# A graph-attention and aggregation kernel: words gathered ahead of a scatter, last tiles turned between products, dense tiles finished between the last gathered ones

## The chip, the cores and the metric

The kernel runs on one core of one Trainium2 chip. The metric is the device time of one execution in microseconds (us). Engines are named as the profile names them: PE (TensorE, matrix products; PEld are its weight loads), DVE (VectorE), ACT (ScalarE), POOL (GpSimd, which here issues all indirect DMAs) and SP (SyncE, which here only issues DMAs). Each engine works through its own instructions in the order written; they meet at semaphores.

## What is computed

Two layers over 4096 nodes with 512 features. The adjacency matrix is 4096 x 4096, symmetric, with about one entry in 500 and the diagonal set. Layer 0 is an attention in which each head takes only its best neighbour; layer 1 is a mean over the neighbours with two linear maps.

```python
h = maximum(layernorm(x), 0)
Q, K, V = h @ WQ.T, h @ WK.T, h @ WV.T            # 8 heads of 64
attn = softmax(Q K^T / 8 + Q @ we.T + be, where adj > 0)
hard = (attn == max(attn, axis=-1)) / 8
x = x + hard @ V

h = maximum(layernorm(x), 0)
agg = mask(adj) @ h / maximum(degree, 1)
self_f, nb_f = h @ W_self + b_self, agg @ W_nb + b_nb
x = x + relu(concatenate([self_f, nb_f]) @ W_comb + b_comb)
```

## The kernel before

Every row of the adjacency matrix is first packed into 256 words of 16 bits; the set bits are decoded into lists of neighbours, and the nodes are sorted by degree into 32 tiles of 128 rows (`perm` holds the permutation). Tile 0 has the nodes of highest degree; `CAPS` holds the length of the longest list of each tile, the node itself included, from 24 for tile 0 to 8 for tile 23, 7 for tiles 24 to 27, 6 for 28 to 30 and 5 for 31. The work has three stages, and in all of them the order of instructions on each engine is the order in which the program writes them (`manual_schedule`).

**First stage** (the first gather of key rows starts at 346.9 us): keys, values, packed words and lists of all tiles.

**Second stage** (to about 1072 us): a loop over `i` from -5 to 31 that takes one tile per round in the order `turns`, which ends with 29, 30, 31. POOL gathers the key rows of the tile's neighbours (L1103), DVE multiplies them with the query and picks the best neighbour of each head (`scores`, `winners`), and the result goes through layer 1's normalisation on ACT (`layer1_stats`, `layer1_norm`), is turned by four PE transposes (`layer1_turn`, into `tr`), copied by ACT (L1347, for the tail L1509), multiplied with the two folded weights on PE, and one product `pg` (= h W_nb W_comb of the tile) is copied by ACT to `gs` and scattered by POOL into the DRAM tensor `G_d` (L1119). The other product goes into `own`, which SP stores with `xo` in `X1_d`. A planner (`plan`) sets in which round each step of each tile comes. The last five tiles, 15, 28, 29, 30 and 31, have no round left for their products; they are the `tail`. For these the steps are: `layer1_turn` (PE), `tail_turn` (ACT copy into `room`, L1509), `tail_product` (PE, eight records of `pg`, L628), `tail_move` (ACT copy to `gs`, L1519, then POOL's scatter). Tiles 15, 28 and 29 are turned in round 30 and multiplied in round 31 (`early`), tile 30 is turned in round 31 and tile 31 after the loop. In round 30 POOL also gathers the packed words of the seven densest tiles (`dense_words`, seven indirect DMAs from `W_d`); they are turned on PE after the loop into `wT`. After that the `own` products of the tail follow.

**Third stage** (from about 1072 us): the neighbour sums of layer 1, in two ways side by side. For the seven *dense* tiles (0 to 6) PE multiplies a 0/1 mask with all of `G`, in 16 planes of 14 products each: per plane DVE unpacks a mask `mk` from `wT` (L1643, three buffers), ACT's queue loads a slab `gk` of `G_d` (three buffers), and PE adds into seven PSUM tiles `da` (L1662). In the last plane the products are sorted by tile, so that tile 0 is complete first. For the *gathered* tiles 7 to 31 POOL gathers the rows of `G_d` of all neighbours (L1103, `CAPS` - 1 gathers of 128 rows, into one of three parts of `room`), and DVE adds them up (`total`, L1684; for tile 31 `halved`, L1693). `finish` is two DVE instructions (L1674, L1675) that scale the sum, add the own product, apply the relu and add x; it reads the tile of `X1_d` that SP loaded (L1669, twelve buffers that are used in turn). `put` is POOL's scatter of a finished tile to the output (L1119); two puts in a row have a small memset between them (L1118). Before the change POOL puts one tile in each round after the round's gathers, and always leaves the latest in the list `done`. Masks are emitted at a pace of one per 13 rows of lists; mask 14 follows tile 23's finish and mask 15 tile 25's, each ahead of the next tile's sum. The seven dense tiles are finished at the end: tiles 0 to 2 after tile 30's sum, before tile 31's, and tiles 3 to 6 after it.

Of the kernel before, what the change touches and what calls it, by code (L numbers as in the profile page):

```python
# [515 lines left out]
DENSE = 7  # L516
# [21 lines left out]
def sparse_path(  # L538
# [553 lines left out]
    with ExitStack() as pb:  # L1092
# [403 lines left out]
        def late(step, kind, i, *args):  # L1496

            out_ = []
            for r in turns:
                if plan[kind].get(r) == i:  # L1500
                    out_ += step(r, *args) or []
            return out_
# [22 lines left out]
        for i in range(-5, KT):  # L1525


            if i == -3:
                load_fold(0)
            if i == 0:  # L1530
                load_bias()
            if i == 1:
                wS = wp.tile([P, NC, D], F32, tag="w_b", name="swS")
                wN = bp.tile([P, NC, D], F32, tag="swN", name="swN", bufs=1)
            a, b = on(key_gathers, i), late(value_gathers, "value", i)
            while a or b:
                for q, n in ((a, max(1, round(len(a) / max(1, len(b))))), (b, 1)):
                    for g in q[:n]:
                        gather(*g)
                    del q[:n]  # L1540
            on(rows, i + 5)
            late(layer1_move, "move", i)
            on(query_copy, i + 2)
            late(layer1_copy, "layer1", i)
            early = [r for r in tail if plan["turn"][r] == i - 1]
            for r in early:
                tail_turn(r)
            if i >= 0 and turns[i] in fused:
                own_values(turns[i])
            late(layer1_stats, "stats", i)  # L1550
            on(query_norm, i + 4)
            on(query, i + 1)
            for part in between.get(i, ()):
                fold(*part)
            late(layer1, "layer1", i)
            for r in early:
                tail_product(r)
            if i in (-2, -1, 0):
                n = 2
                for t in late_v[:n]:  # L1560
                    w = values_out(t, values(t, psm), bp, nc.sync)
                    for g in beyond:
                        tc.declare_no_dep(w.ins, g.ins, reason="other columns")
                    written.append(w)
                del late_v[:n]
            if i == max(between) + 1:
                fold_bias()

            def within():
                late(layer1_inverse, "stats", i)  # L1570
                late(layer1_out, "move", i)

            if i >= 0:
                scores(turns[i], within)
            late(scatter, "move", i)
            if i == KT - 2:
                wg = dense_words()
                gsl = [gp.tile([P, GRP, D], F32, tag="kg", name="gs") for _ in range(2)]
            on(winners, i)
            late(layer1_norm, "stats", i)  # L1580
            on(query_turn, i + 3)
            late(layer1_turn, "turn", i)
            for r in early:
                tail_move(r)

        late(layer1_xo, "stats", KT)
        for r in tail:
            if plan["turn"][r] == KT - 1:
                tail_turn(r)
                tail_product(r)  # L1590
        late(layer1_stats, "stats", KT, True)
        late(layer1_norm, "stats", KT)
        for r in tail:
            if plan["turn"][r] == KT - 1:
                tail_move(r)
        for r in tail:
            if plan["turn"][r] == KT:
                layer1_turn(r)
                tail_turn(r)
                tail_product(r)  # L1600
                tail_move(r)


        over = bp.tile([P, KT], F32, tag="over", name="over", bufs=1)
# [26 lines left out]
    with ExitStack() as pd:  # L1631
        dp = pd.enter_context(tc.tile_pool(name="sd", bufs=4))
        gp = pd.enter_context(tc.tile_pool(name="sdg", bufs=3))
        psd = pd.enter_context(tc.tile_pool(name="spsd", bufs=1, space=PSUM))
        order = pd.enter_context(ExitStack())
        order.enter_context(tc.manual_schedule())
        dacc = [psd.tile([P, D], F32, tag=f"da{r}", name="da") for r in range(DENSE)]
        masks, keys = {}, {}

        def dense_mask(s):  # L1640

            mk = gp.tile([P, 2, DENSE, P], F32, tag="mk", name="mk")
            nc.vector.tensor_scalar(  # L1643
                mk.rearrange("p h b q -> p (h b q)").bitcast(I32),
                wT.rearrange("p h b q -> p (h b q)"), 22 - s, 0x40000000,
                ALU.logical_shift_left, ALU.bitwise_and,
            )
            masks[s] = mk

        def dense_keys(s):  # L1650
            gk = gp.tile([P, 2, D], F32, tag="gk", name="gk")
            nc.scalar.dma_start(
                gk, G_d[ds(s * SEG, SEG), :].rearrange("(h p) f -> p h f", p=P)
            )
            keys[s] = gk

        def dense_sum(s):
            todo = [(h, r) for h in range(2) for r in range(DENSE)]
            if s == NPL - 1:
                todo.sort(key=lambda hr: hr[1])  # L1660
            for h, r in todo:
                nc.tensor.matmul(  # L1662
                    dacc[r], masks[s][:, h, r, :], keys[s][:, h, :],
                    start=(s == 0 and h == 0), stop=(s == NPL - 1 and h == 1),
                )

        def load_x1(r):
            x1 = dp.tile([P, 2, D], F32, tag="x1", name="x1", bufs=DENSE + 5)
            nc.sync.dma_start(x1, X1_d[ts(r, P), :, :])  # L1669
            return x1  # L1670

        def finish(r, acc, by, x1):
            x1, y = x1[:, 0, :], x1[:, 1, :]
            nc.vector.scalar_tensor_tensor(y, acc, by, y, ALU.mult, ALU.add)  # L1674
            nc.vector.scalar_tensor_tensor(y, y, 0.0, x1, ALU.max, ALU.add)  # L1675
            done.append((r, y))

        def put():
            put_rows(out[:, :], *done.pop(0))

        def total(g, n):

            acc = dp.tile([P, D], F32, tag="acc", name="acc", bufs=2)
            nc.vector.tensor_reduce(  # L1684
                acc, g[:, 0:n, :].rearrange("p n f -> p f n"), AX.X, ALU.add
            )
            return acc

        def halved(g, n):

            while n > 1:
                h = n // 2
                nc.vector.tensor_tensor(  # L1693
                    g[:, 0:h, :], g[:, 0:h, :], g[:, n - h : n, :], ALU.add
                )
                n -= h
            return g[:, 0, :]


        half = cp.tile([P, DENSE], F32, tag="half", name="half")  # L1700
        nc.vector.tensor_scalar(half, smeta[:, 0:DENSE, M_RD - M_DEG], 0.5, None, ALU.mult)
        done = []
        puts.clear()
        for s in range(NPL):
            dense_keys(s)
        ahead = 3
        for s in range(ahead):
            dense_mask(s)
            dense_sum(s)
        s = ahead  # L1710
        calls = 0

        pace = 13
        x1s = {}
        for r in range(DENSE, KT):
            n = CAPS[r] - 1
            for q in [*range(r, min(r + 4, KT)), *(range(DENSE) if r == KT - 2 else ())]:
                if q not in x1s:
                    x1s[q] = load_x1(q)
            gg = room[:, ds(r % 3 * GMAX * D, GMAX * D)].rearrange("p (n f) -> p n f", f=D)  # L1720
            for i in range(n):
                gather(gg[:, i, :], G_d[:, :], sidx[:, r, i + 1 : i + 2])
            if len(done) > 1:
                put()
            if r == KT - 1:

                for k in range(DENSE // 2):
                    finish(k, dacc[k], half[:, k : k + 1], x1s.pop(k))
                    put()
            acc = (total if r < KT - 1 else halved)(gg, n)  # L1730
            finish(r, acc, smeta[:, r, M_RD - M_DEG : M_RD + 1 - M_DEG], x1s.pop(r))
            calls += n + 1
            while s < NPL and calls >= pace * (s - 2):
                dense_mask(s)
                dense_sum(s)
                s += 1
        while done:
            put()
        for k in range(DENSE // 2, DENSE):
            finish(k, dacc[k], half[:, k : k + 1], x1s.pop(k))  # L1740
            put()
        order.close()
    return nc.values_load(fi[0:1, 0:1], min_val=0, max_val=P)  # L1743
# [46 lines left out]
```

## Time and profile before

| | |
|---|---|
| median of 5 runs | 1429.41 us (1425.88 to 1443.62) |
| the profiled execution | 1414.95 us |
| its span, first to last instruction | 1413.1 us |
| first gather of G (third stage) | at 1072.70 us |
| first mask of the dense products | at 1110.27 us |
| PE's last dense product ends | at 1377.7 us |
| DVE's last finish ends, POOL's last put starts | at 1400.20, 1400.48 us |

The rows of a timeline give the start and the duration in us, the engine, the line, the operation with the tile it writes and those it reads, the shapes, the count of instructions that are merged in the row, and in brackets the idle time of the engine before it with what ended that. "issue" means that nothing in the profile shows what the engine waited for, "remote" a release by something that could not be named. A product of 128x512 in float32 leaves two records on PE. Starts and ends of PE records are not exact: the record is that of the issue, and the end is modelled.

### The profile page before, as it was taken

Reading aid. Unit: us, or ns where it says so; the run is one execution under the profiler, and the core shown is the slowest. Engines: PE = TensorE matmul, PEld = TensorE weight load, DVE = VectorE, ACT = ScalarE, POOL = GpSimd, SP = SyncE. Lnnn points to the kernel's source line nnn. Section 1 sums busy time; section 2 is a strip of 40 time slices with the busy share of each in tenths; the row PEclk is TensorE's granted clock in tenths of the full one; section 3 lists DMA queues with packets and bytes.
Section 4 is the critical chain, followed back from the end, with each engine's and each line's share of the span. In section 5 each row is a group of like instructions: output and inputs, shape, how many; then the busy total and the mean of one; then the engine's idle time right before and its main releaser. Section 6 shows DMA issues by size and latency. Waiting matters only on the chain. (4 is left out here: it accounts for less than half of the span.)

```text
span 1413.1 us, 10657 instructions
## 1 busy us (share of the span) xinstructions
PE 1045.1 (74%) x2852; PEld 475.9 (34%) x2852; DVE 997.7 (71%) x1651; ACT 427.7 (30%) x880; POOL 782.6 (55%) x918
## 2 busy tenths in 40 slices
PE   5998989858772648567787757777789397887590
PEld 3554545423330223223332223333333143333140
DVE  5468786884594398778877787777572577688395
ACT  5787776612100333232333323332530000000000
POOL 2222313233677476666766666667345475767474
PEclk9999999979985769778887888888899698979595
DMA  9999998296765376777777777767555896778673
GB/s 364 419 420 421 420 361 304 109 352 218 210 202 152 97 240 216 227 233 244 224 229 225 221 226 225 225 208 223 209 175 173 306 332 220 256 253 276 206 235 124
DMA packets 109973, 352.57 MB, mean 249 GB/s; under 512 B 18208, under 2 KB 18208, under 8 KB 101712
## 3 DMA queue, kind: packets, MB, share of 16 engines
q0 software_dynamic: 64128, 210.72, 47.3%
q1 hardware_dynamic: 39552, 129.78, 23.8%
q10 hardware_dynamic: 6224, 11.31, 2.3%
q8 instruction: 24, 0.39, 0.1%
q14 instruction: 45, 0.37, 0.1%
HBM read 287.74 MB, written 68.19 MB: 252 GB/s over the span
## 5 line engine op out<-in xcount | busy, mean ns | idle before, releaser
L1662 PE MATMUL da<-gk,mk 128*128 128x512 f32 x448 | 215.0, 633 | 67.9 <-issue 45.6
L628 PE MATMUL q<-wq,hqT 128*128 128x512 f32 x256 | 147.8, 691 | 120.7 <-issue 100.0
L1103 POOL DMA_INDIRECT room<-G_d,sidx x184 | 184.3, 1002 | 57.8 <-issue 54.8
L1103 POOL DMA_INDIRECT kg<-K_d,sidx x177 | 169.9, 960 | 75.8 <-issue 54.3
L1227 DVE TENSOR_REDUCE sc<-pr 128x32 f32<-128x2048 f32 (+3 forms) x114 | 183.3, 1608 | 3.9
L1684 DVE TENSOR_REDUCE acc<-room 128x512 f32<-128x4096 f32 (+5 forms) x24 | 161.1, 6713 | 7.6 <-DMA room<-G_d,sidx 6.5
L628 PE MATMUL pg<-swN,hT 128*128 128x512 f32 x216 | 127.9, 747 | 45.2 <-ACT hT L1347 40.1
L1662 PEld LDWEIGHTS da<-gk,mk 128*128 128x128 f32 x448 | 90.2, 202 | 192.8 <-issue 192.8
L1103 POOL DMA_INDIRECT o<-K_d,vi x128 | 123.6, 966 | 39.2 <-issue 38.7
L628 PE MATMUL pk<-wk,room 128*128 128x512 f32 x256 | 118.3, 605 | 4.5 <-ACT room L810 4.4
L1103 POOL DMA_INDIRECT room<-K_d,sidx x102 | 99.3, 974 | 32.9 <-issue 26.8
L628 PE MATMUL pv<-wv,room 128*128 128x512 f32 x256 | 116.8, 608 | 0.0
L628 PEld LDWEIGHTS q<-wq,hqT 128*128 128x128 f32 x256 | 51.9, 213 | 184.9 <-issue 179.6
L1224 DVE TENSOR_TENSOR pr<-q,kg 128x2048 f32<-128x2048 f32 (+3 forms) x51 | 102.4, 2007 | 1.3
L1360 PE MATMUL pr<-swS,hT 128*128 128x512 f32 x216 | 99.9, 605 | 0.0
L1224 DVE TENSOR_TENSOR pr<-q,room 128x2048 f32<-128x2048 f32 (+3 forms) x42 | 66.8, 1590 | 41.1 <-issue 26.5
L628 PEld LDWEIGHTS pg<-swN,hT 128*128 128x128 f32 x216 | 50.9, 244 | 129.6 <-issue 69.7
L1119 POOL DMA_INDIRECT G_d<-gs,perm x32 | 31.8, 993 | 101.9 <-ACT gs L1366 68.4
L1366 ACT COPY gs<-pg 128x512 f32<-128x512 f32 x27 | 15.7, 583 | 223.2 <-remote 134.7
L749 ACT ACTIVATE mkt<-adjt,sgb 128x2048 bf16<-128x2048 int32 x37 | 74.2, 2006 | 13.3 <-POOL adjt L670 13.1
L1260 DVE COPY_PREDICATED o<-best,room 128x512 f32<-128x512 int32 x102 | 74.3, 729 | 4.6 <-DVE o L1260 1.1
L824 POOL DMA_DIRECT2D K_d<-ks x32 | 18.8, 587 | 100.8 <-DVE ks L819 98.6
(222 smaller groups left out, 1537.1 us busy)
## 6 DMA issues: line engine op xcount, KB each, us to landing
adjt<-adj_dram SPq DMA_DIRECT2D x37, 1024.0 KB
room<-adj_dram SPq DMA_DIRECT2D x27, 1024.0 KB
x<-X_d SPq DMA_DIRECT2D x32, 512.0 KB
xt<-x_dram SPq DMA_DIRECT2D x32, 256.0 KB
K_d<-ks POOLq DMA_DIRECT2D x32, 256.0 KB
X_d<-xo SPq DMA_DIRECT2D x32, 256.0 KB
X_d<-own SPq DMA_DIRECT2D x32, 256.0 KB
gk<-G_d ACTq DMA_DIRECT2D x16, 512.0 KB
```

The lines of the kernel that those rows point to most:

```text
L628: nc.tensor.matmul(dst, h[:, c, :], w[:, c, :], start=(c == 0), stop=(c == NC - 1))
L749: nc.scalar.activation(mk, st[t]["adj"][j], AF.Sigmoid, bias=sgb, scale=400.0, accum_out=degs[:, t, j : j + 1],)
L824: nc.gpsimd.dma_start(K_d[ts(t, P), D : 2 * D], ks)
L1103: last[0] = nc.gpsimd.indirect_dma_start(out=dst, out_offset=None, in_=src, in_offset=bass.IndirectOffsetOnAxis(ap=idx, axis=0), element_o ...
L1119: new = nc.gpsimd.indirect_dma_start(out=dst, out_offset=bass.IndirectOffsetOnAxis(ap=perm[:, r : r + 1], axis=0), in_=src, in_offset=None,)
L1224: nc.vector.tensor_tensor(pr[:, :g, :], s["q"].unsqueeze(1).to_broadcast([P, g, D]), kk, ALU.mult)
L1227: nc.vector.tensor_reduce(sc[:, g0 : g0 + g, :], pr[:, :g, :].rearrange("p g (h d) -> p g h d", h=H), AX.X, ALU.add,)
L1260: nc.vector.copy_predicated(s["o"].rearrange("p (h d) -> p h d", h=H), best[:, k, :].bitcast(I32).unsqueeze(2).to_broadcast([P, H, HD]), b ...
L1360: nc.tensor.matmul(pr, s["hT1"][:, c, :], wS[:, c, :], start=False, stop=(c == NC - 1))
L1366: nc.scalar.copy(s["gs"], s["pg"])
L1662: nc.tensor.matmul(dacc[r], masks[s][:, h, r, :], keys[s][:, h, :], start=(s == 0 and h == 0), stop=(s == NPL - 1 and h == 1),)
L1684: nc.vector.tensor_reduce(acc, g[:, 0:n, :].rearrange("p n f -> p f n"), AX.X, ALU.add)
```

## The change

It has three parts. In round 30 `dense_words` is called before the scatter of that round, and no longer after it. The tail is reordered: in round 31 only the first two of the early tiles are multiplied; tile 30 is turned and copied after these, ahead of the product of tile 29, and tile 31's statistics, which end with a root on ACT, and its norm come before the copy of tile 29's product; tile 31 is turned before tile 30's product. Last, the dense tiles are finished two after tile 27, two after tile 28 and three after tile 29, ahead of the next tile's sum; POOL puts up to two tiles in rounds 29 and 30 and all that are waiting in round 31; and SP loads the dense tiles' rows of `X1_d` in the round of tile 26 instead of that of tile 30.

```diff
@@ -1553,7 +1553,7 @@
             late(layer1, "layer1", i)
-            for r in early:
+            for r in early[: -1 if i == KT - 1 else None]:
                 tail_product(r)
...
@@ -1572,33 +1572,39 @@
             if i >= 0:
                 scores(turns[i], within)
+            if i == KT - 2:
+                wg = dense_words()
             late(scatter, "move", i)
             if i == KT - 2:
-                wg = dense_words()
                 gsl = [gp.tile([P, GRP, D], F32, tag="kg", name="gs") for _ in range(2)]
             on(winners, i)
             late(layer1_norm, "stats", i)
             on(query_turn, i + 3)
-            late(layer1_turn, "turn", i)
-            for r in early:
-                tail_move(r)
-
+            if i < KT - 1:
+                late(layer1_turn, "turn", i)
+                for r in early:
+                    tail_move(r)
+
+        before, at_end = ([r for r in tail if plan["turn"][r] == k] for k in (KT - 1, KT))
+        for r in early[:-1]:
+            tail_move(r)
+        for r in before:
+            layer1_turn(r)
+            tail_turn(r)
+        for r in early[-1:]:
+            tail_product(r)
         late(layer1_xo, "stats", KT)
-        for r in tail:
-            if plan["turn"][r] == KT - 1:
-                tail_turn(r)
-                tail_product(r)
         late(layer1_stats, "stats", KT, True)
         late(layer1_norm, "stats", KT)
-        for r in tail:
-            if plan["turn"][r] == KT - 1:
-                tail_move(r)
-        for r in tail:
-            if plan["turn"][r] == KT:
-                layer1_turn(r)
-                tail_turn(r)
-                tail_product(r)
-                tail_move(r)
+        for r in early[-1:]:
+            tail_move(r)
+        for r in at_end:
+            layer1_turn(r)
+            tail_turn(r)
+        for r in before + at_end:
+            tail_product(r)
+        for r in before + at_end:
+            tail_move(r)
...
@@ -1714,30 +1720,28 @@
             n = CAPS[r] - 1
-            for q in [*range(r, min(r + 4, KT)), *(range(DENSE) if r == KT - 2 else ())]:
+            for q in [*range(r, min(r + 4, KT)), *(range(DENSE) if r == KT - 6 else ())]:
...
-            if len(done) > 1:
-                put()
-            if r == KT - 1:
-
-                for k in range(DENSE // 2):
-                    finish(k, dacc[k], half[:, k : k + 1], x1s.pop(k))
+
+            for k in range(len(done) if r == KT - 1 else 2 if r in (KT - 3, KT - 2) else 1):
+                if len(done) > (r < KT - 1):
                     put()
             acc = (total if r < KT - 1 else halved)(gg, n)
             finish(r, acc, smeta[:, r, M_RD - M_DEG : M_RD + 1 - M_DEG], x1s.pop(r))
+
+            for k in {KT - 5: (0, 1), KT - 4: (2, 3), KT - 3: range(4, DENSE)}.get(r, ()):
+                finish(k, dacc[k], half[:, k : k + 1], x1s.pop(k))
             calls += n + 1
             while s < NPL and calls >= pace * (s - 2):
                 dense_mask(s)
                 dense_sum(s)
                 s += 1
+        assert s == NPL
         while done:
-            put()
-        for k in range(DENSE // 2, DENSE):
-            finish(k, dacc[k], half[:, k : k + 1], x1s.pop(k))
             put()
```

## The prediction

> **What bounds the kernel now.** The profiled execution took 1414.95 us, of which 1413.1 are its span. It is 14.5 us under the median of the five timed runs (1429.41) and 10.9 under the lowest of them, so a timed run holds some 11 to 29 us of waiting that this profile does not show. I read the page's busy times first: no engine is full over the span, so the bound must be sought stage by stage.
>
> ```profile
> PE 1045.1 (74%) x2852; PEld 475.9 (34%) x2852; DVE 997.7 (71%) x1651; ACT 427.7 (30%) x880; POOL 782.6 (55%) x918
> ```
>
> Then the timelines of the two places that the diff touches. At the seam between the stages (1010 to 1075 us), PE:
>
> ```profile
> 1046.92 12.16 PE L628 MATMUL pg<-swN,room 128*128 128x512 f32 x24
> 1058.92 0.60 PE L1138 MATMUL tr<-sid,hn 128*128 128x128 f32 x4
> 1060.25 3.70 PE L628 MATMUL pg<-swN,room 128*128 128x512 f32 x8 [0.72 <-ACT room L1509]
> 1063.78 0.60 PE L1138 MATMUL tr<-sid,hn 128*128 128x128 f32 x4
> 1065.11 3.70 PE L628 MATMUL pg<-swN,room 128*128 128x512 f32 x8 [0.73 <-ACT room L1509]
> ```
>
> Five tail products (tiles 15, 28, 29 in the first line, then 30, then 31) run end to end but for two gaps in which PE waits for ACT to copy the turned tile. Tile 31's product is copied, scattered at 1069.71, and the first gather of G starts at 1072.70. POOL, in the same stage and in the next:
>
> ```profile
> 1024.55 1.00 POOL L1119 DMA_INDIRECT G_d<-gs,perm  x1 [12.86 <-ACT gs L1366]
> ...
> 1123.86 1.01 POOL L1119 DMA_INDIRECT out_dram<-x,perm  x1 [13.60 <-DMA x<-X_d]
> ```
>
> In the dense stage the chain that ended last runs through DVE's masks and sums; its longest piece is a wait for a mask buffer, which the products of an earlier plane set free:
>
> ```profile
> 1313.92 0.69 DVE x L1675
> 1314.61 21.58 another core or an unknown queue
> ...
> 1399.51 0.70 DVE x L1675
> ```
>
> PE's rows of that time and DVE's of the end:
>
> ```profile
> 1248.42 49.93 PE L1662 MATMUL da<-gk,mk 128*128 128x512 f32 x112 [0.39 <-issue]
> 1300.43 0.59 PE L1662 MATMUL da<-gk,mk 128*128 128x512 f32 x1 [2.07 <-issue]
> ...
> 1334.72 43.00 PE L1662 MATMUL da<-gk,mk 128*128 128x512 f32 x93 [1.08 <-issue]
> ```
>
> ```profile
> 1365.61 4.57 DVE L1684 TENSOR_REDUCE acc<-room 128x512 f32<-128x2560 f32 x1
> ...
> 1372.94 4.56 DVE L1684 TENSOR_REDUCE acc<-room 128x512 f32<-128x2560 f32 x1 [1.25 <-DMA room<-G_d,sidx]
> ...
> 1381.13 4.47 DVE L1684 TENSOR_REDUCE acc<-room 128x512 f32<-128x2560 f32 x1 [2.12 <-DMA room<-G_d,sidx]
> ...
> 1387.04 0.74 DVE L1674 SCALAR_TENSOR_TENSOR x<-da,half,x 128x512 f32<-128x512 f32 x1
> ```
>
> PE records come every 0.45 us (49.93/112), but from 1300 to 1335 only 13 appear in 34.3 us, 2.6 us each. DVE waited three times for mask buffers (18.83, 16.36 and 21.61 us), each beside such a slow stretch. So PE drags DVE, and DVE drags POOL (14.46 us before the put at 1344.41). After the last slow stretch PE ends at 1377.7, and DVE finishes gathered tiles, then dense ones, to 1400.20.
>
> **Words gathered ahead of the scatter.** The seven gathers of words took POOL from 1025.85 to 1034.39. Now they fill the 12.86 us in which POOL waited for ACT, so tile 31's four gathers start at 1025.85 instead of 1034.70, 8.85 us earlier; their buffer is free (DVE's predicated copies of tile 29 read it from 1022.64 to 1026.43, in the same order). The scatter is not late: 7 x 1.26 = 8.8 is less than 12.86. DVE's wait of 3.69 us for these gathers goes. What is late next: after the first sum of scores DVE takes a reciprocal that needs ACT's statistics of tile 30, which end at 1049.69, and DVE was there at 1050.12. ACT is late because its copy of turned tile 15 began at 1045.79 after waiting 7.45 us for PE, not for POOL. So 0.4 us off DVE, none of it on PE's path. Bounds: 0, and 2.9 (0.4 plus the 2.5 from the transposes' last record, 1043.27, to that copy) if ACT's wait also shrinks. I take 0, the row that names PE.
>
> **Tail order.** PE now does pg15, pg28, turn 30, pg29, turn 31, pg30, pg31. The copy of turned tile 30 (0.59) lies beside pg29 (8 records, 3.5 us), that of 31 beside pg30, so both gaps close: 0.72 + 0.73 = 1.45 us. Tile 31 must be normed when pg29 ends, at 1046.92 + 24 x 0.43 + 1.7 for a slow start + 0.4 for turn 30 = 1059.4. Its statistics are ready at 1057.17; the root was at 1060.08 only because two copies stood before it on ACT, and now one does, ending near 1057.0; root to normed took 2.2 us (1060.08 to 1062.30), so 1059.4: a tie. If the tie is lost, 1 us of the gain is. ACT's copy of product 29 now waits behind that norm, and behind it its scatter, some 0.6 us; the scatters of 30 and 31 come 4 and 8 us later, so that is hidden. Taken: -1.45; bounds -0.4 and -1.9 (both gaps and the odd tenths around them). The first gather of G moves with it, and so do the five own products and the start of the dense stage.
>
> **Dense finishes between the last gathered ones.** A finish is 1.38 us from start to start (1387.04 to 1388.42). Nothing is removed; seven finishes move from after tile 30's sum to after tiles 27, 28 and 29. They can fill DVE's two waits for gathers: 1371.61 to 1372.94 and 1378.94 to 1381.13, 3.5 us together. But each now stands, in DVE's order, before the next sum, and needs PE's last plane. That plane goes tile by tile, 4 records each, so tile 0 is complete 24 records before PE's end: 1377.7 - 24 x 0.43 = 1367.4, and tile 1 at 1369.1. DVE comes at 1365.61. Chain: tile 0 at 1367.45 (1.84 waited), tile 1 at 1369.15 (0.3 waited), to 1370.55; sum and finish of 28, 6.0, to 1376.6; two dense, 2.8, to 1379.3; tile 29, 6.0, to 1385.4; three dense, 4.2, to 1389.5; tile 30, 5.9, to 1395.4; tile 31, 3.45 (1391.20 to 1394.65), to 1398.9. Before it was 1400.20: -1.3 us. The gathers of 28 to 31 have landed by then (the last one landed 3.5 us after its issue). POOL is moved past one more put in each of two rounds, 1.38 us each, ahead of the gathers of 30 and 31; DVE comes to these 8 and 4 us later than before, which hides it; without that cover it would cost the 2.8. Before the gathers of 30 POOL now also waits for tile 0's finish, near 1368.9; it is there at 1371.2. The last seven puts lie beside DVE's last sums. SP's seven loads of dense x1 wait for puts two tiles earlier than they did (buffers turn in order), and the loads for tiles 30 and 31 go behind them, free at the puts of 1353.67 and 1361.77, 30 us before use: nothing.
>
> The rows put the loads beside a POOL that stood idle from 1330 to 1344, with the DMA share at 0.56. [...]
>
> Sum: -1.45 - 1.3 = -2.75 us: 1412.2 for the profiled execution, 0.2%, so 1426.6 beside the median.
>
> **Rivals.** (A) Slower: PE is late when DVE stands at the first dense finish, and DVE idles with three sums behind it that need no PE. Before, DVE had these 18 us of sums to do first. When mask 15 has waited for plane 12, DVE needs 1.0 + 2 x 6.85 = 14.7 us to reach dense tile 0, and PE 60 records, 25.8 us: 11 us idle, and the end some 10.5 later than before, less 1.45: +9, 1438.5. When a slow stretch falls in the last three planes, the old end is PE's end + 3 (one finish and one put) and the new one PE's end + 22: tile 1 is complete 8.6 us before PE's end, and behind it stand 1.4 + 6.0 + 2.8 + 6.0 + 4.2 + 5.9 + 3.5 and a put of 1, 30.8. That is +19, less 1.45, 1447. It decides from a PE some 4 us later, against DVE, than in this profile. For it: slow stretches took 11, 20 and 34 us of the 260 that PE spent here, and the timed runs are longer. Against it: in this profile the last 41 us before PE's end have none.
>
> The row is 2.6 us per record from 1300 to 1335. [...]
>
> (B) Faster: the last own product's records end at 1094.74 but DVE, waiting for it, went on at 1106.28, 11.5 us late, and the masks followed at 1110.27. If the new order moves that lateness away, the dense stage starts up to 11 us sooner and POOL's 13.60 us wait shrinks with it: 1426.6 - 11 = 1415.6. Against it: nothing in the diff removes PE work. (C) The hoisted gathers do shorten ACT's wait: -2.9 more, 1424; inside the forecast's own range.
>
> **How the numbers follow.** Runs of this kernel differ by 1.2%, so about 1% is what a measurement can tell from no change. Forecast with C: 0.54, 1426.6, own range 1418 to 1433. A: 0.30, 1434 to 1450; above 1443.7 it is over 1%, which takes a slow stretch near the end, and as they held a quarter of PE's time here I give that 0.22 of the 0.30. B: 0.16, 1405 to 1418, of which 0.14 lies below 1415.1. So faster 0.14, same 0.64, slower 0.22. Range 1411 to 1447: out are the worst third of A and the best half of B.
>
> **What would show it.** No ACT-made gap before the products of 30 and 31; words before the scatter, and no DVE wait for tile 31's gathers; DVE's waits for gathers at the end gone, and in their place waits at the finishes that read da: near 2 us if I am right, over 6 for A. Wrong if the three slow stretches change in number or length by more than 10 us.

## The result, and the profile after

The changed kernel took 1428.16 us in the median of 46 runs (1404.12 to 1462.29), the kernel before 1428.88 in 88 runs beside it (1407.60 to 1457.54). These medians are 0.05% apart; among the runs within 1.5% of the fastest of their kernel, which leaves out more than half of both, the ratio is 0.9962, 95% interval [0.9938, 0.9987]: 0.4% faster, 5.4 us of 1429 (1.9 to 8.9). On another chip the same kernel gave 0.9937 [0.9898, 0.9977]. So there is a small gain, clearer on the second chip than on the first, and smaller than the 1% that the prediction took as its bound: no change by that measure, and inside the range.

The profiled execution of the changed kernel took 1428.09 us. Single executions spread over some 50 us, and the profile shown of before was one of the shortest of its kernel. So the two spans are not to be subtracted; what can be compared between two profiles are stretches between two fixed events in each. Two such stretches carry this case: the **seam**, from the scatter of tile 26 to the first gather of G, and the **end**, from the start of DVE's sum of tile 27 to the end of the last put.

The page of the changed kernel, span and busy times:

```profile
span 1426.3 us, 10657 instructions
...
PE 1043.4 (73%) x2852; PEld 475.0 (33%) x2852; DVE 997.2 (70%) x1651; ACT 428.2 (30%) x880; POOL 782.5 (55%) x918
```

No engine does more or less than before. The timeline of the seam (start, length, engine, line, operation, and in brackets the idle time before it and its releaser):

```profile
1021.73 0.95 POOL L1103 DMA_INDIRECT wg<-W_d,perm  x1 [0.30 <-issue]
1023.19 0.99 POOL L1119 DMA_INDIRECT G_d<-gs,perm  x1 [0.51 <-issue]
1024.49 0.97 POOL L1103 DMA_INDIRECT room<-K_d,sidx  x1 [0.30 <-issue]
...
1041.57 1.07 ACT L1509 COPY room<-tr 128x512 f32<-128x512 f32 x2 [4.53 <-PE tr L1138]
...
1042.70 7.27 PE L628 MATMUL pg<-swN,room 128*128 128x512 f32 x16
1049.81 0.60 PE L1138 MATMUL tr<-sid,hn 128*128 128x128 f32 x4
1050.25 3.60 PE L628 MATMUL pg<-swN,room 128*128 128x512 f32 x8
1054.71 0.65 PE L1138 MATMUL tr<-sid,hn 128*128 128x128 f32 x4 [0.87 <-ACT hn L1338]
1055.20 7.03 PE L628 MATMUL pg<-swN,room 128*128 128x512 f32 x16
```

The words now end just as the scatter comes due (0.51 us idle, where POOL had waited 12.86), and tile 31's gathers follow it at once. The two gaps in which PE waited for a copy are gone, and in place of them PE waits 0.87 us for tile 31's norm. And one thing has changed that the diff does not name: ACT waits 4.53 us for the turned tiles 15 and 28, where it had waited 7.45 with a releaser that the profile could not name. These are the rows of the kernel before, the copy and the transposes that it needs:

```profile
1042.23 1.04 PE L1138 MATMUL tr<-sid,hn 128*128 128x128 f32 x8
...
1045.79 1.07 ACT L1509 COPY room<-tr 128x512 f32<-128x512 f32 x2 [7.45 <-remote]
```

The end of the changed kernel's profile:

```profile
1285.27 53.85 PE L1668 MATMUL da<-gk,mk 128*128 128x512 f32 x121 [0.39 <-issue]
1375.24 17.30 PE L1668 MATMUL da<-gk,mk 128*128 128x512 f32 x37 [0.39 <-issue]
...
1382.28 0.75 DVE L1680 SCALAR_TENSOR_TENSOR x<-da,half,x 128x512 f32<-128x512 f32 x1 [17.80 <-PE da L1668]
...
1384.00 0.75 DVE L1680 SCALAR_TENSOR_TENSOR x<-da,half,x 128x512 f32<-128x512 f32 x1 [0.24 <-PE da L1668]
...
1385.39 4.57 DVE L1690 TENSOR_REDUCE acc<-room 128x512 f32<-128x2560 f32 x1
...
1412.10 0.75 DVE L1680 SCALAR_TENSOR_TENSOR x<-room,smeta,x 128x512 f32<-128x512 f32 x1
...
1369.94 1.00 POOL L1119 DMA_INDIRECT out_dram<-x,perm  x1 [0.30 <-issue]
1370.92 0.13 POOL L1118 MEMSET gap<- 128x1 f32 x1
1384.04 0.99 POOL L1119 DMA_INDIRECT out_dram<-x,perm  x1 [12.99 <-DVE x L1681]
```

DVE stands for 17.80 us at the first dense finish, because PE's third slow stretch lies late here: between 1339 and 1375 only 18 records appear. PE ends at 1392.5, and 22 us later, at 1414.8, the last put ends, with three sums of 4.5 us in between that need nothing of PE. The two waits for gathers at the end, 1.25 and 2.12 us before, are gone.

### The profile page after: what moved, and what is told of

The parts are those of the page before. It is cut to its first block, busy times and chain, and to the rows that moved or that the text cites. A ratio compares the mean times of both kernels' runs of the same rounds, so it can differ in the third digit from the quotient of the medians.

```text
span 1426.3 us, 10657 instructions
## 1 busy us (share of the span) xinstructions
PE 1043.4 (73%) x2852; PEld 475.0 (33%) x2852; DVE 997.2 (70%) x1651; ACT 428.2 (30%) x880; POOL 782.5 (55%) x918
## 5 line engine op out<-in xcount | busy, mean ns | idle before, releaser
L1668 PE MATMUL da<-gk,mk 128*128 128x512 f32 x448 | 223.5, 646 | 80.9 <-issue 56.8
L628 PE MATMUL q<-wq,hqT 128*128 128x512 f32 x256 | 143.2, 680 | 106.1 <-issue 76.7
L1103 POOL DMA_INDIRECT room<-G_d,sidx x184 | 184.1, 1000 | 57.9 <-issue 54.2
L628 PE MATMUL pg<-swN,hT 128*128 128x512 f32 x216 | 121.9, 717 | 69.1 <-ACT hT L1347 65.3
L1103 POOL DMA_INDIRECT o<-K_d,vi x128 | 123.2, 963 | 39.2 <-issue 38.1
L749 ACT ACTIVATE mkt<-adjt,sgb 128x2048 bf16<-128x2048 int32 x37 | 74.2, 2006 | 13.1 <-POOL adjt L670 12.1
L1119 POOL DMA_INDIRECT out_dram<-x,perm x32 | 34.7, 1085 | 73.0 <-DVE x L1681 65.7
```

The costliest lines, as they stand in the source:

```text
L628: nc.tensor.matmul(dst, h[:, c, :], w[:, c, :], start=(c == 0), stop=(c == NC - 1))
L749: nc.scalar.activation(mk, st[t]["adj"][j], AF.Sigmoid, bias=sgb, scale=400.0, accum_out=degs[:, t, j : j + 1],)
L1103: last[0] = nc.gpsimd.indirect_dma_start(out=dst, out_offset=None, in_=src, in_offset=bass.IndirectOffsetOnAxis(ap=idx, axis=0), element_o ...
L1119: new = nc.gpsimd.indirect_dma_start(out=dst, out_offset=bass.IndirectOffsetOnAxis(ap=perm[:, r : r + 1], axis=0), in_=src, in_offset=None,)
L1668: nc.tensor.matmul(dacc[r], masks[s][:, h, r, :], keys[s][:, h, :], start=(s == 0 and h == 0), stop=(s == NPL - 1 and h == 1),)
```

## The experiments

Twelve runs were made, two of them repeats. Line numbers shift by a few between the kernels. First, each part of the change alone, in one set of runs on one chip (before there: 1438.95 us).

**Words alone.** The hoist of the diff and nothing else:

```diff
+            if i == KT - 2:
+                wg = dense_words()
             late(scatter, "move", i)
             if i == KT - 2:
-                wg = dense_words()
```

> Only the words are gathered ahead of the scatter. My theory (PE and ACT set the seam, POOL does not): 0 us from the tail itself, at most -2.9; DVE's wait of 3.7 us for tile 31's gathers is gone, the copy of turned tile 15 starts when PE has turned it; ratio 0.998 to 1.002. Rival (the hoist carries the measured gain of 0.4%, because ACT's 7.45 us wait was POOL's work after all): the first gather of G 4 to 6 us earlier than 1072.7, ratio 0.996 or less.

Measured: 1432.24 us, 0.995 [0.9917, 0.9983], and a seam of 43.8 us where before has 48.2: the rival's numbers, not the theory's. It is the part that pays.

**Tail order alone.** All lines of the diff from `early[: -1 ...` to the last `tail_move`, the rest as before.

> Only the tail is reordered. My theory: the gaps of 0.72 and 0.73 us before the products of tiles 30 and 31 go, a wait of up to 0.9 us for tile 31's norm takes their place, so from the first tail product to the last copy it takes 0.6 to 2 us less; ratio 0.997 to 1.001. Rival (the order carries the whole gain): 4 us or more from the first product to the last copy, ratio 0.996 or less.

Measured: 1440.49 us, 1.0028 [0.9991, 1.0066], a seam of 46.4. From the first tail product to the last copy it is 2.3 us less, a little more than expected, and no gain in time is to be seen.

**Both, with the dense finishes where they were.**

> The whole change without the moved dense finishes, which stand at the end as before. My theory: this has the gain of the seam (1 to 5 us) and none of the exposure at the end, so it is as fast as the changed kernel or faster: ratio 0.993 to 0.998. Rival (the finishes bring the gain): 1.000, and the changed kernel beats it by 0.3% or more.

Measured: 1430.51 us, 0.9962 [0.9931, 0.9994], a seam of 43.2: the new order adds only half a microsecond to what the hoist brings.

**Dense finishes alone.** The last hunk of the diff, on the kernel before.

> Only the dense finishes (with their puts and loads) are moved. My theory: -1.3 us where PE's last plane is in time, up to +18 where a slow stretch of PE falls into the last planes; over runs the two about cancel: ratio 0.998 to 1.006, and the runs spread more than those of the kernel before. Rival (the finishes bring the gain): ratio 0.996 or less. In the profile: the wait before the first finish that reads da is 1 to 20 us, according to where the last slow stretch of PE ends.

Measured: 1445.18 us, 1.0052 [1.0016, 1.0087]: alone it makes the kernel slower, by 7.5 us (2.3 to 12.5). Its timeline shows the wait:

```profile
1393.80 0.75 DVE L1674 SCALAR_TENSOR_TENSOR x<-da,half,x 128x512 f32<-128x512 f32 x1 [8.29 <-remote]
```

Then four runs on a further chip (before there: 1431.20 us).

**The change, and the change without the moved finishes, side by side.** The first is the changed kernel, the second is the kernel of `words_tail` again.

> The changed kernel once more, beside words_tail2 (the same without the moved dense finishes) on one chip. Theory 1, from the four single edits: seam 48.2 to 43.1 us (scatter of tile 26 to the first gather of G), and the moved finishes wait for PE's last plane and cost 0 to 0.5%: ratio to before 0.996 to 1.000, and 0 to 6 us more than words_tail2. Theory 2, the prediction's sum: the finishes gain 1.3 us, so 1 to 2 us less than words_tail2.

> Hoisted words and new tail order, dense finishes where they were before. Theory 1 (finishes cost something, the seam gives 5.1 us): ratio to before 0.9955 to 0.998 and not above that of after2. Theory 2 (finishes gain 1.3 us): 1 to 2 us above after2.

Measured: 1425.73 us, 0.9937 [0.9898, 0.9977], and 1424.93 us, 0.992 [0.9886, 0.9954]. Both ratios are below theory 1's ranges. The moved finishes cost 0.8 us by the medians, as theory 1 has it, but these intervals can't tell that from nothing or from a gain. Both profiles have PE late at the end. In the changed order DVE waits 20.30 us at the first dense finish; in the old order it waits too:

```profile
1398.14 0.75 DVE L1680 SCALAR_TENSOR_TENSOR x<-da,half,x 128x512 f32<-128x512 f32 x1 [6.54 <-PE da L1668]
...
1401.55 0.75 DVE L1680 SCALAR_TENSOR_TENSOR x<-da,half,x 128x512 f32<-128x512 f32 x1 [1.94 <-PE da L1668]
```

These are rows of the second kernel. All sums but the halved one of tile 31 stand ahead of its first dense finish, so of the lateness only 8.8 us are left.

**Why the hoist helps.** The hoist, and the seven gathers issued a second time at the old place:

```diff
+            if i == KT - 2:
+                wg = dense_words()
             late(scatter, "move", i)
             if i == KT - 2:
-                wg = dense_words()
+                dense_words()
```

(against the kernel before; it is the first set that is used, not the second as the expectation has it).

> Words hoisted ahead of the scatter, and the same seven gathers issued a second time behind it, at the old place, into a further buffer of the same name that then is the one used; nothing else is changed. So the scatter stands as in the hoisted kernel, but tile 31's four key gathers leave POOL as late as before. Theory 1 (the turned tile 15 comes late to ACT because tile 31's 2 MB of key gathers land at that moment): ACT's copy of turned tile 15 starts over 2 us after the end of PE's last transposes again, and from the scatter of tile 26 to the first gather of G it is 48 us as before. Theory 2 (what helped is only the earlier words, or less work behind the scatter): the copy starts within 0.5 us of the transposes' end and the stretch is 43.7 us as with the hoist alone.

Measured: one run of 1435.23 us. The copy of turned tile 15 came on time, yet the seam was 54.2 us, longer than both numbers. The timeline says where:

```profile
1039.87 0.96 POOL L1103 DMA_INDIRECT o<-K_d,perm  x1 [0.30 <-issue]
1045.79 1.00 POOL L1119 DMA_INDIRECT G_d<-gs,perm  x1 [4.96 <-ACT gs L1366]
...
1045.26 2.29 DVE L1224 TENSOR_TENSOR pr<-q,room 128x2048 f32<-128x2048 f32 x1 [3.14 <-DMA room<-K_d,sidx]
...
1027.83 3.60 PE L628 MATMUL pg<-swN,hT 128*128 128x512 f32 x8
...
1035.94 3.60 PE L628 MATMUL pg<-swN,hT 128*128 128x512 f32 x8
1045.56 2.07 PE L1358 MATMUL pr<-sbb,s 1*128 1x512 f32 x2 [6.02 <-ACT gs L1366]
...
1044.92 1.07 ACT L1366 COPY gs<-pg 128x512 f32<-128x512 f32 x2 [6.95 <-remote]
```

ACT copies two products here. PE's records of the first end at 1031.43, those of the second at 1039.54. ACT, which waits for the first, goes on at 1044.92, 13.5 us after its end (5.4 after that of the second) and 4.1 after POOL's last gather. The lateness that theory 1 looked for at one completion of PE fell on earlier ones. So theory 1 had the cause in the right place (the run of gathers) and named the wrong victim; theory 2 had the copy right and the stretch wrong by 10 us.

**Is PE slow by its own load?** The second half of every dense plane's products left out, masks and keys still made:

```diff
-            todo = [(h, r) for h in range(2) for r in range(DENSE)]
+            todo = [(h, r) for h in range(1) for r in range(DENSE)]
```

(and `stop` at the first half of the last plane).

> The kernel before with the second half of every dense plane's products left out: the masks and key planes are still made, so DVE, ACT, POOL and the DMAs do all they did and PE does half of its dense work (some 100 us of records in place of 195). Theory 1 (PE's own load makes the three slow stretches, and they make DVE wait 15 to 22 us each for mask buffers): no slow stretch or a short one, no mask wait over 5 us, the dense stage some 20 to 45 us shorter, span 1370 to 1395 beside 1413 to 1440. Theory 2 (gathers' DMA traffic makes them): stretches of 2 us and more per record still there, with the same lengths of 14, 27 and 40 us; the span falls by under 15 us.

Measured: one run of 1396.02 us, span 1394.1. The span is theory 1's, the cause isn't: with half the work there is still a stretch, from 1256.8 to 1273.9, with records 1.4 to 2.8 us apart, and DVE waits 20.35 us for a mask buffer in it.

```profile
1260.62 1.01 PE L1662 MATMUL da<-gk,mk 128*128 128x512 f32 x1 [0.82 <-issue]
1263.41 1.01 PE L1662 MATMUL da<-gk,mk 128*128 128x512 f32 x1 [1.78 <-issue]
1266.21 1.01 PE L1662 MATMUL da<-gk,mk 128*128 128x512 f32 x1 [1.79 <-issue]
1269.01 1.01 PE L1662 MATMUL da<-gk,mk 128*128 128x512 f32 x1 [1.79 <-issue]
...
1283.73 1.09 DVE L1643 TENSOR_SCALAR mk<-wT 128x1792 int32<-128x1792 int32 x1 [20.35 <-remote]
...
1282.22 0.95 POOL L1103 DMA_INDIRECT room<-G_d,sidx  x1 [0.30 <-issue]
1292.73 0.99 POOL L1119 DMA_INDIRECT out_dram<-x,perm  x1 [9.56 <-DVE x L1675]
```

The order of events is to be seen here: PE's records stand 2.8 us apart while POOL gathers; POOL issues its last gather at 1282.22, and its next instruction, a put, waits for DVE; 1.5 us after that gather's start DVE has its mask buffer from PE.

**With nearly no gathers.** This run and the three below are of one more chip (before there: 1429.71 us). One gather for each gathered tile:

```diff
-            for i in range(n):
+            for i in range(1):
                 gather(gg[:, i, :], G_d[:, :], sidx[:, r, i + 1 : i + 2])
```

> The kernel before with only one gather of G for each gathered tile; the sums of these tiles then read what the buffer held before, so their outputs mean nothing, and DVE does as many sums as before. The dense stage has a tenth of its gather traffic, and POOL pauses after each gather. Theory 1 (PE's products come late while POOL issues gathers one after another): no slow stretch, PE's records every 0.43 to 0.45 us but for waits at plane starts, no wait of DVE for a mask buffer over 5 us. Theory 2 (the stretches come from PE alone, as a limit on its use): stretches with records 2 us and more apart still there, 10 us or longer.

Measured: one run of 1336.75 us. Theory 1, to the letter. All 448 records of the dense products stand in one row of the timeline, 0.44 us each:

```profile
1105.98 195.31 PE L1662 MATMUL da<-gk,mk 128*128 128x512 f32 x448 [8.19 <-DMA gk<-G_d]
```

and DVE's waits in the dense stage come to

```profile
DVE mk L1643 <- DMA X_d<-own: 2.3, 1, 2.3
DVE mk L1643 <- PE da L1662: 0.2, 1, 0.2
```

(total, times, longest). So the slow stretches come with the gathers, and not from what PE itself does; that is one run.

**PE's last planes taken away.** Products of planes 13 to 15 left out, on both orders of the finishes:

```diff
+            if s > NPL - 4:
+                return
...
-            if s == NPL - 1:
+            if s == NPL - 4:
```

> Hoisted words and new tail order, finishes where they were before, and the products of the last three dense planes (13 to 15) left out, their masks and keys still made: PE is done some 36 us sooner than DVE needs it, so no finish waits for it. Measured in the profile from the start of the sum of tile 27 to the end of the last put; in the four profiles with this order and PE in time it is 42.7 to 42.9 us. Both theories: 42.9 us. It is the base for early_after.

> The changed kernel with the same products of the last three planes left out. Theory 1 (what the moved finishes cost is only their wait for PE's last plane): with PE in time the wait at the first dense finish is under 1 us, and from the sum of tile 27 to the last put it is 41.6 us, 1.3 less than early_wt, as the prediction worked out; in after2, with the wait, it was 59.7. Theory 2 (the loads of x1 and the puts moved ahead of the last gathers cost time too): no wait, and still 43 us or more.

Measured: single runs of 1414.66 and 1414.36 us; 44.0 us from the sum of tile 27 to the last put in the old order, 51.1 in the new one. The second run did not do what it was made for: PE was late even with 36 us less to do.

```profile
1348.75 1.01 PE L1670 MATMUL da<-gk,mk 128*128 128x512 f32 x1 [1.79 <-issue]
...
1369.06 0.75 DVE L1682 SCALAR_TENSOR_TENSOR x<-da,half,x 128x512 f32<-128x512 f32 x1 [12.12 <-remote]
...
1361.85 0.99 POOL L1119 DMA_INDIRECT out_dram<-x,perm  x1 [0.30 <-issue]
1362.84 0.12 POOL L1118 MEMSET gap<- 128x1 f32 x1
1370.82 0.98 POOL L1119 DMA_INDIRECT out_dram<-x,perm  x1 [7.86 <-DVE x L1683]
```

PE's last record is issued at 1348.75. DVE stands ready for it from 1356.9, POOL stops at 1362.96, and DVE goes on at 1369.06. Of 51.1 us, 12.1 are that wait; 39.0 are left, which is used below.

**Two buffers for the gathers where there were three.** The kernel of `words_tail`, with

```diff
-            gg = room[:, ds(r % 3 * GMAX * D, GMAX * D)].rearrange("p (n f) -> p n f", f=D)
+            gg = room[:, ds(r % 2 * GMAX * D, GMAX * D)].rearrange("p (n f) -> p n f", f=D)
```

> Hoisted words and new tail order, finishes as before, and two buffers for gathered rows in turn where there were three, so POOL runs out of free buffers one tile (9 to 18 us) sooner when DVE waits for a mask buffer. Theory 1 (PE's completions are held back while POOL issues gathers without a pause, and are let go when it stops; in three of the profiles the mask wait ended 1 to 6 us after such a stop): the longest wait for a mask buffer falls from 16 to 22 us to under 12, the slow stretches get shorter, and the time is between 10 us less and 3 us more than words_tail2. Theory 2 (PE slows for itself, and POOL's stop is only a consequence): mask waits of 15 us and more stay, and the time is 0 to 15 us above words_tail2.

Measured: 1426.65 us, 1.000 [0.9957, 1.0042] against before. The longest wait for a mask buffer is 18.2 us, so theory 1's number failed. The time, 1.7 us above that of `words_tail2` on another chip, lies in the range of both theories. The order of events is still that of theory 1:

```profile
1182.72 1.09 DVE L1649 TENSOR_SCALAR mk<-wT 128x1792 int32<-128x1792 int32 x1 [18.22 <-remote]
...
1192.04 1.36 POOL L1103 DMA_INDIRECT room<-G_d,sidx  x1 [14.00 <-DVE acc L1690]
```

POOL had stopped at 1178.04, 4.7 us ahead of the mask. A buffer less does not bring that stop early enough to help. DVE waits more for gathers (22.0 us in the dense stage, 4.4 in `words_tail2`), which may be where the gain of the seam is spent.

## Why the prediction was right, and where it was wrong

The forecast was 0.2% faster and 0.4% was measured. That the total came out near is luck: two terms were off in opposite directions. These are the two stretches, in us, in every profile but those with half the products and with a tenth of the gathers:

```
                 seam    end    of which DVE waits for PE's last products    end less wait
before           48.2    42.7   0                                            42.7
tail             46.4    42.9   0                                            42.9
words            43.8    42.9   0                                            42.9
words_tail       43.2    42.9   0                                            42.9
words_tail2      43.2    52.6   8.8                                          43.8
words_pad        54.2    48.3   4.9                                          43.4
room2            44.5    44.1   0                                            44.1
early_wt         42.0    44.0   0                                            44.0
finish           48.4    47.5   8.3                                          39.2
after            43.1    57.2   18.0                                         39.2
after2           42.9    59.7   20.5                                         39.2
early_after      42.9    51.1   12.1                                         39.0
```

**Words: the mis-sized term.** The step reads "I take 0, the row that names PE", between bounds of 0 and 2.9. Measured alone it is 4.4 us of seam, and 0.995 in time. What was predicted of it happened: the words fill POOL's wait, the scatter isn't late, DVE's 3.69 us for tile 31's gathers are gone. What failed is the reading of the row. Its releaser reads "remote", one that could not be named, and the prediction took it for PE at work. The semaphore that the copy waits for is PE's, but PE's last transposes had ended at 1043.27, 2.5 us ahead of the copy, and the four that it needs at 1042.84. The prediction saw the 2.5 us and put them in a bound.

The trace has the moments at which PE's semaphore rises: in the kernel before 164 of the 265 recorded rises come within 0.02 us of the end of a record that raises it, though not every rise is recorded (313 records raise it). Three rises of that profile stand at 1045.71, 1045.77 and 1045.83, 0.06 us apart, for records that had ended at 1042.40, 1042.84 and 1043.27, so 2.6 to 3.3 us late. POOL had issued without a pause from 1024.55 to 1043.28: scatter, words, tile 31's gathers, two scatters. With the hoist POOL pauses (0.51 us before the scatter in the changed kernel and 3.83 in `words`, and 4.3 behind tile 31's gathers in `words` and in `after2`), and the rises come one by one and on time: in `words` at 1054.61, 1055.05 and 1055.49. The profiles agree on this without exception: in the five without the hoist (`before`, `tail`, `finish`, `light_before`, `no_gather`) the copy starts 2.6 to 3.2 us after the end of its transposes, in the nine with it 0.03. `words_pad`, which makes the run of gathers longer, moves the lateness to earlier products: rises at 1044.90, 1045.03 and 1045.13, where the product that ACT waits for had ended at 1031.43.

So 2.9 us of the gain lie ahead of ACT's copy of turned tile 15 (21.2 us after the scatter before, 18.3 in `words`), and 1.5 in the products behind it: in the kernel before PE stood idle for 3.2 us ahead of product 15, the granted clock was 0.5 from 1047.1 to 1050.5, and PE's records in that time stood 0.85 us apart. Rival C was this case, priced at 2.9 with no such slow start in it.

Over a whole execution no pair of profiles shows the gain. From the scatter of tile 26 to the last put it is 377 us in `before`, 384 in `tail`, 389 in `finish`, and 386 to 391 in `words`, `words_tail` and `words_tail2`: the slow stretches of the dense stage vary by more than the seam gives. That the hoist makes the kernel faster rests on the timed runs. Whether it also lengthens the slow stretches is not shown.

The end in a row and the rise are two moments: an end of 1043.27 and a rise of 1045.83 belong to the same record. The difference is anything from 0.01 us to 20 and more here (in `early_after` PE's last record ends at 1349.76, and the rise of its tile stands at 1370.08).

**Tail order: right.** The gaps before the products of 30 and 31 are gone in every kernel with the new order. From the start of product 15 to the copy of product 31 it is 21.9 us before and 19.6 after. Beside the hoist, which had shortened the same stretch to 20.5, it is worth 0.9, and 0.5 of the seam. The predicted 1.45 lies between that and the 1.7 of the seam that it brings alone. The tie for tile 31's norm was lost by 0.87 us, the "1 us of the gain" that the text allowed for.

**Dense finishes: the chain right, PE's place in it wrong.** The prediction let DVE wait 1.84 and 0.3 us for PE, and came to 1.3 us less. Without its waits that chain makes an end of 42.7 - 1.3 - 2.1 = 39.3 us. In four profiles it measures 39.0 to 39.2, against 42.7 to 44.1 in the old order: the moved finishes do fill the waits for gathers, and the puts and loads that were moved cost nothing that shows. They pay as long as PE is less than some 3.6 us late. But PE was 8.3 to 20.5 us late in all four, and then rival A is what happens, its bound ("from a PE some 4 us later") included. In `after` and `after2` the last put ends 22.3 us after PE's last dense record, the "PE's end + 22" of that rival. The failed step is the sentence "in this profile the last 41 us before PE's end have none", taken as a reason for the 1.84 and 0.3. One profile showed where PE's last slow stretch had fallen once. Measured back from PE's last record, it ends 42 to 47 us before in `tail`, `words`, `words_tail` and `finish` as well, but 35 in `room2` and only 8 to 19 in `after`, `after2`, `words_tail2` and `words_pad`; of `words_tail` and `words_tail2`, which are one kernel, the first has 42 and the second 12. And even with 47 us free of slow stretches in `finish`, DVE waits 8.3: 5.0 for PE's records of tile 0, which end at 1390.46, and 3.3 for the rise, at 1393.77. The prediction's own signs tell the same: it gave "over 6 for A", and "Wrong if the three slow stretches change in number or length by more than 10 us". The wait is 18 us, and the stretches are about 25, 38 and 38 us in the changed kernel, 12, 22 and 37 before; this change of length cannot be put down to the edit on one profile each, since the stretches of `words_tail` and `words_tail2`, the same kernel, differ by 6 to 13 us.

The price of the moved finishes is not the full 14 to 17 us that the wait takes from the table. In `after` and `after2` the stretch from the first gather of G to the sum of tile 27 is 291 us, in `words` and `words_tail`, where PE came in time at the end, 304 and 302 (286 in `before`, so this stretch varies for other reasons too): it looks as if a lateness that DVE would have met at a mask buffer were met at the first finish instead, which these few profiles don't prove. Over the whole dense stage, to the last put, the changed kernel's two profiles take 348.5 and 351.2 us, and 343.2 to 346.8 is what `words`, `words_tail` and `words_tail2` take, so 2 to 8 us more. In time the moved finishes cost 0.5% alone, and beside the hoist it stays open whether they cost anything: 0.9937 and 0.992 overlap.

**Rival B** gave the changed order up to 11 us for the last own product, which DVE gets late. It did not happen: from the fourth to the fifth own sum it is 16.1 us before and 21.0 after. In `no_gather` it is 4.7 us, so that lateness too comes with the gathers, which the change leaves alone.

**What makes PE late.** In the twelve profiles with all gathers and at least 13 planes of full products there are 34 slow stretches of 8 us or more after which PE had records left. Each of them ended between 2 and 6 us after POOL had stopped issuing for 3 us or more. POOL stops there because its next put waits for a tile that DVE has not finished (14.42 us in the changed kernel, to 1295.15; in `room2` its next gather waits 14.00 us for a buffer that DVE has not read); DVE stands at a mask buffer (24.44 us in the changed kernel, to 1286.06); and DVE stands there because PE is slow. `no_gather` shows that the gathers are needed for it, `light_before` that half of PE's own load gone does not end it (there PE waits for masks and keys as well, so its stretches can't be counted the same way). That the stop lets PE go is read from the order of events alone; the run that was to bring the stop forward, `room2`, did not shorten the waits.

Two things in the traces say that the news of finished work is late, and not only the work. In `early_after` the rises of six dense tiles stand 0.06 us apart, from 1369.78 to 1370.08, where the four records of a tile take 1.7 us. And the lateness is not PE's alone: in `words_pad` ACT, which at the rows below waits for nothing but its own instruction before, goes on 1.1 us after that instruction's end, where 0.03 or 0.04 us is usual (ahead of the same two lines at 1058.47 and 1058.80 in that run). Its starts are then 1.40 us apart, twice the 0.70 us of which the distances of PE's slow records are multiples (see the last section).

```profile
1034.35 0.30 ACT L1327 ACTIVATE q<-q 128x1 f32<-128x1 f32 x1 [0.25 <-ACT q L1326]
1035.75 0.29 ACT L1328 ACTIVATE q<-q 128x1 f32<-128x1 f32 x1 [1.10 <-issue]
1037.16 0.81 ACT L1329 ACTIVATE hn<-xo,q 128x512 f32<-128x512 f32 x1 [1.11 <-ACT q L1328]
```

What in a gather holds the others back, its issue on POOL or its data, isn't settled. A high DMA share alone does not do it: in `words` it was 0.98 from 1043 to 1047, and PE's rise at 1045.41 came 0.02 us after the record's end, 1.4 us after POOL had paused; in the kernel before it was 0.89 in that time, with rises up to 3.3 us late. Nor does the share differ much between a slow and a fast stretch, as the windows of the changed kernel show (busy us and count of PE, PEld, DVE, ACT, POOL, then granted clock, DMA share, GB/s):

```profile
1285.00:1339.00 54.00, 53.73 (x121) 23.64 (x121) 50.29 (x23) 0.00 (x0) 34.10 (x33) 0.96 0.69 229
1339.00:1375.00 36.00, 16.27 (x18) 4.21 (x16) 20.45 (x10) 0.00 (x0) 24.74 (x26) 0.56 0.76 262
```

The granted clock falls to 0.56 in the slow stretch, but at half clock records stood 0.85 us apart (in the seam, above), and these are 2 us apart. The clock falls to 0.5 only at 1343.5, 5 us after the stretch begins at 1338.5, so it is not the cause. A slow stretch did fall near the last planes, which is the case that rival A had named.

Gathers do hold PE up here: 448 records take 195 us with a tenth of the gathers (`no_gather`), and 261 to 293 in the ten profiles with all of them and all planes. Where they do so isn't shown.

No version here clearly beats the changed kernel. The hoist and the new tail order with the finishes left in place had 0.9962 and 0.992 on two chips, the whole change 0.9962 and 0.9937; they are the same within the intervals, and so is the hoist alone (0.995), which needs three lines of the diff.

## What to carry to other kernels

When you put a wait down to an engine, above all where the row says "remote", compare the end of that engine's last record with the moment at which the waiting engine goes on. A difference of microseconds isn't explained by the rows of either, and its cause is worth looking for in what runs beside both (here, an unbroken run of indirect DMAs from 1024.55 to 1043.28, with rises 2.6 to 3.3 us late behind it). Break such runs where there is a wait to put them in. And do not move work that needs the last result of an engine ahead of work that doesn't, on the word of one profile: ask first how far the end of that engine moves from profile to profile.

## What the runs showed of the hardware that was not expected

- PE's semaphore rises came several at once and some 3 us or more after the end of the record, behind an unbroken run of indirect DMAs on POOL: at 1045.71, 1045.77 and 1045.83 in the kernel before for ends of 1042.40 to 1043.27, at 1044.90, 1045.03 and 1045.13 in `words_pad`, where the first product waited for had ended at 1031.43.
- In `words_pad` ACT went on 1.1 us late, at 1035.75 and 1037.16, when it waited only for itself.
- In the slow stretches PE's records start at multiples of 0.70 us from one another: in the changed kernel's profile 44 of the 447 distances between starts of dense records are 1.4, 2.1, 2.8 or 3.5 us, where 381 are 0.43 us.
- PE's dense records stood 0.44 us apart for 195 us without a break once nine tenths of the gathers were gone (`no_gather`), at a granted clock of 0.99; half of PE's own work taken away did not bring that about (`light_before`: records 1.4 to 2.8 us apart from 1256.8 to 1273.9).
